# A two-layer graph attention kernel: streamed weights, block loads and weight negations moved in the queues of its first superblock

## The chip, the cores and the metric

The kernel runs on one core of one Trainium2 chip. The metric is the device time of one execution in microseconds; a comparison takes the median of several. In the profile, PE is TensorE (PEld its weight loads), DVE is VectorE, ACT is ScalarE, POOL is GpSimd and SP is SyncE, whose queue (SPq) issues nearly all DMAs. "L530" is line 530 of the kernel before.

## The reference

`x` is 128 graphs of 64 nodes with 768 features, in float32; `adj` is 128 symmetric 64x64 masks with ones on the diagonal. Cut to what matters:

```python
h = relu(layernorm(x))
for l in range(2):
    m_left, m_right = h @ W_left[l].T, h @ W_right[l].T
    u_left  = einsum('bih,bjh->bij', h, m_left) / sqrt(768)
    u_right = einsum('bih,bjh->bij', h, m_right) / sqrt(768)
    u = u_left * triu(adj) + u_right * triu(adj, 1).T
    e = exp(u) * adj
    attention = e / (sum(e, axis=2) + 1e-10)
    ctx = attention @ (h @ W_lin[l].T + b_lin[l])
    h = relu(layer_norm(ctx, ln_a[l], ln_b[l]))
out = x + h
```

## The kernel before

**Tiling.** The 8192 tokens are cut into 16 blocks of 512 (four pairs of graphs on each half), two blocks form a superblock, so there are 8 superblocks. For each layer two passes run. Pass one computes the projections with W_left and W_right and, from them, the scores and the softmax, which it stores in DRAM as the transposed attention. Pass two computes the projection with W_lin, then the context, its norm and either the next layer's rows (layer 1, stored in DRAM) or the output (layer 2).

**The products.** Both passes multiply by a scheme of fast matrix multiplication (blocks of 256 by 256): pass one has 29 products for a superblock (`PRODUCTS`, index i from 0 to 28) instead of 36. Each product takes a sum of weight blocks, made by `W_OPS`, and a sum of token blocks, made by `X_OPS` on GpSimd (token index 12 and up). Each product has two runs of eight matmuls, k = 0 for the left weights and k = 1 for the right ones. A run takes about 1.73 us. Results are accumulated in PSUM banks X, Y, Z for k = 0 and V, right0, right1 for k = 1, and read into the tile `m` (`read`, L293): the first time an output block appears ScalarE copies it (L303), later VectorE adds (L221). A bank may not be written again until its reads have run.

**The weights.** In superblock 0 of layer 1 the weight sums are made while the products run: those of the left on VectorE, most of those of the right on GpSimd (`weight_op`, L180 to L186). `W_OPS` has two negations for each side, weights 16 and 27, used by products 7 and 20. The sums lie in tiles that are free at the time, handed out by `Singles`: a list of groups, each with a limit; a tile of a group takes only weights whose last use is at or before the group's limit. After product i its two weights are kept in DRAM (`keep_weight`, L194). From superblock 1 on the weights are streamed (L197) from there into a ring of 8 tiles of 512 KB, each an l and r pair. The first five streamed tiles go into ring tiles that superblock 0 uses for single weights, so they can't start before these are dead (L698 to L700). Later streams are sent by `streamed` (L554), and around the scores they are held back (`HELD`, and a small copy on ScalarE at L558 that the next stream waits for), so that the DMA queue is quiet while the scores run.

**The rows.** Layer 1's blocks 0 and 1 come in by TensorE transposes. For blocks 2 and up `load_rows` (L360) loads rows of `x`; `transpose_rows` (L384) then queues four statistics on VectorE (L338, L339), the scale (ScalarE L407, VectorE L408 and L409), four normalisations with Relu on ScalarE (L412) and four 32x32 transposes on VectorE (L397), then the store to DRAM (L394). `load_h` (L371) brings the block back with features on the partitions. Block 3 is written out by hand (L731 to L740), since the first half of its rows has a tile of its own.

**The order.** It is written out by hand. A superblock of pass one has 116 slots: four for each product (after the first four matmuls and at the end of the two runs: slots 4i, 4i+1, 4i+2, 4i+3). `put(slot, f)` plans f for a slot, `put_all` a list of them with a step, and `run(slot)` issues what is planned; a slot with nothing planned takes the next of the `idle` list. Within an engine instructions run in the order of issue. SyncE issues DMAs in program order too, and as it runs nothing else it is often ahead of TensorE. `starts` (L751 to L755) gives the slots at which the two next blocks begin.

**The scores.** `scores` (L460, L472) multiplies the tokens of a block by `m`: 192 short matmuls of 32 columns of weights into the bank `both`. In superblock 1 those of block 0 come after product 0, those of block 1 after product 2. The chain of a block's softmax (`chain`, L476 to L512) is cut into steps by `yield`: mask products on VectorE (L488), their sum (L492), Exp on ScalarE (L494), the row sums and the division (L496 to L502), a transpose (L506) and eight small stores. At the end of pass one the last block's chain is planned into the first slots of pass two (L793), beside the first products of `linear` (L1049, L1063).

**Layer 2.** Its pass one takes the right banks from the memory that pass two of layer 1 used for its context, so product 0's second run waits for the last norm of that pass (L1032, L1034).

## Time and profile before

| | us |
|---|---|
| median of 3 runs | 2712.75 |
| lowest, highest | 2711.25, 2714.27 |
| the profiled execution | 2710.28 |
| its span | 2708.5 |

The stretches of the span, with the busy time of each engine in it:

| stretch, us | what runs | PE | DVE | ACT | POOL | DMA share |
|---|---|---|---|---|---|---|
| 0 to 10 | load, first transposes | 7.12 | 5.50 | 5.04 | 1.05 | 0.84 |
| 10 to 60 | layer 1, superblock 0 | 47.96 | 38.77 | 27.80 | 31.64 | 0.87 |
| 60 to 130 | the same, and the start of superblock 1 | 64.32 | 49.39 | 4.08 | 47.47 | 0.78 |
| 130 to 240 | superblock 1 | 107.91 | 69.83 | 25.62 | 37.41 | 0.87 |
| 240 to 780 | superblocks 2 to 6 | 539.10 | 320.77 | 134.52 | 204.15 | 0.72 |
| 880 to 910 | end of pass one, start of pass two | 27.72 | 18.94 | 6.36 | 25.12 | 0.13 |
| 910 to 1330 | layer 1, pass two | 420.00 | 153.52 | 200.10 | 258.54 | 0.56 |
| 1330 to 1380 | its end, start of layer 2 | 48.11 | 13.58 | 26.67 | 18.28 | 0.73 |
| 1380 to 2200 | layer 2, pass one | 819.87 | 429.64 | 171.72 | 309.87 | 0.72 |
| 2650 to 2709 | the end | 47.40 | 42.80 | 18.39 | 35.98 | 0.55 |

PE's busy time is read against the length of the stretch: where the two agree, nothing but the matmuls sets the pace. The granted clock of TensorE is 0.999. A line of the timeline gives the start in us, the duration in us, the engine, the line, the operation, what it writes and reads, how many are merged, and in brackets the idle time of the engine just before and what ended it. Tiles bear the names of the memory they lie in: a weight sum in superblock 0 can be `wp` (a ring tile), `ht`, `room`, `bias` or `ts`.

### The profile page before, as it was taken

How to read it: one execution, taken by the hardware profiler on the slowest of the kernel's cores; microseconds unless marked ns; L12 is line 12 of the kernel's file. 1: busy time of each engine (PE TensorE's matmuls, PEld its weight loads, DVE VectorE, ACT ScalarE, POOL GpSimd, SP SyncE). 2: the span in 40 equal slices, each digit the busy share in tenths (PEclk: the TensorE clock that was granted, in tenths of full speed). 3: DMA queues.
4: the chain of work that ended last, by engine and by line, in shares of the span. 5: the costliest groups of instructions: out<-in, count | busy, mean ns of one | idle time of the engine just before them, and what ended most of it. 6: DMA issues, size and time to landing. Idle time of an engine off the chain costs nothing.

```text
span 2708.5 us, 47300 instructions
## 1 busy us (share of the span) xinstructions
PE 2677.3 (99%) x18514; PEld 2304.5 (85%) x18514; DVE 1502.9 (55%) x2458; ACT 829.2 (31%) x1615; POOL 1380.6 (51%) x1071
## 2 busy tenths in 40 slices
PE   9899999999999999999999999999999999999998
PEld 7788888888888888888788888888888888888886
DVE  7665655756647433334343645546446475666667
ACT  4032131321310254454631221221212304445443
POOL 5633244333336776566433325334244286887886
PEclk9999999999999999999999999999999999999999
DMA  8886966858765345558585956958759524655655
GB/s 268 273 304 208 286 204 205 280 203 263 243 209 179 98 144 180 169 168 259 180 279 176 308 190 220 283 185 287 227 194 302 211 79 133 185 157 159 185 156 148
DMA packets 310223, 567.81 MB, mean 210 GB/s; under 512 B 62833, under 2 KB 190065, under 8 KB 301809
## 3 DMA queue, kind: packets, MB, share of 16 engines
q1 hardware_dynamic: 309840, 564.39, 65.1%
q8 instruction: 148, 2.42, 0.4%
q14 instruction: 75, 0.61, 0.1%
q10 hardware_dynamic: 160, 0.39, 0.0%
HBM read 429.40 MB, written 135.27 MB: 208 GB/s over the span
## 4 chain that ended last, share of the span: by engine, by line
PE 94%; DVE 2%; DMA 1%; SPq 1%; issue 0%; ACT 0%; DVEq 0%
PE right L530 17%; PE X L1063 12%; PE X L530 11%; PE V L530 10%; PE Z L530 9%; PE Y L530 9%; PE V L1063 8%; PE Y L1063 6%; PE both L472 5%; PE Z L1063 4%; PE aux L871 2%; PE aux L894 1%; PE Y L894 0%; DMA wp<-ws 0%; PE Z L472 0%
## 5 line engine op out<-in xcount | busy, mean ns | idle before, releaser
L221 POOL TENSOR_TENSOR ts<-ht 128x512 f32<-128x512 f32 x352 | 479.7, 1369 | 160.7 <-PE X L1063 65.9
L221 POOL TENSOR_TENSOR ts<-ht,ts 128x512 f32<-128x512 f32 x192 | 253.0, 1325 | 348.5 <-PE V L530 208.2
L530 PE MATMUL right<-ts,wp 128*128 128x252 f32 (+1 forms) x1632 | 381.1, 377 | 1.5 <-DVE wp L221 1.5
L530 PEld LDWEIGHTS right<-ts,wp 128*128 128x128 f32 x1632 | 310.5, 190 | 40.0 <-DVE wp L221 1.9
L481 POOL TENSOR_TENSOR wm<-adj,tri 128x256 f32<-128x256 f32 x60 | 42.2, 726 | 493.9 <-DMA wp<-ws 220.7
L221 DVE TENSOR_TENSOR m<-m,X 128x512 f32<-128x512 f32 x160 | 105.6, 685 | 259.6 <-ACT m L303 181.3
L221 DVE TENSOR_TENSOR m<-m,right 128x504 f32<-128x504 f32 (+1 forms) x304 | 199.5, 673 | 87.5 <-PE right L530 73.5
L1063 PE MATMUL X<-room,ts 128*128 128x256 f32 x1024 | 244.1, 380 | 0.2
L221 POOL TENSOR_TENSOR ts<-ht,ht 128x512 f32<-128x512 f32 x128 | 163.5, 1288 | 140.0 <-PE right L530 93.7
L530 PE MATMUL Z<-ts,wp 128*128 128x256 f32 x992 | 234.5, 380 | 0.1
L1063 PEld LDWEIGHTS X<-room,ts 128*128 128x128 f32 x1024 | 192.0, 190 | 31.3 <-issue 1.8
L530 PEld LDWEIGHTS Z<-ts,wp 128*128 128x128 f32 x992 | 188.8, 190 | 24.8 <-issue 0.4
L530 PE MATMUL X<-ts,wp 128*128 128x256 f32 x872 | 207.5, 381 | 0.0
L530 PE MATMUL V<-ts,wp 128*128 128x252 f32 (+1 forms) x864 | 201.7, 377 | 0.0
L303 ACT ACTIVATE m<-right 128x504 f32<-128x504 f32 (+1 forms) x64 | 36.1, 590 | 510.2 <-PE both L472 490.3
L380 ACT ACTIVATE ht<-ht,b_col,a_col 128x512 f32<-128x512 f32 x192 | 140.8, 803 | 144.0 <-DMA ht<-h 144.0
L530 PEld LDWEIGHTS X<-ts,wp 128*128 128x128 f32 x872 | 164.9, 190 | 22.8
L1063 PE MATMUL Y<-room,ts 128*128 128x256 f32 x768 | 182.6, 380 | 0.0
L530 PEld LDWEIGHTS V<-ts,wp 128*128 128x128 f32 x864 | 164.4, 190 | 20.2
L1063 PEld LDWEIGHTS Y<-room,ts 128*128 128x128 f32 x768 | 146.1, 190 | 20.1 <-issue 0.6
L221 DVE TENSOR_TENSOR m<-m,Y 128x512 f32<-128x512 f32 x144 | 95.8, 683 | 115.1 <-PE Y L530 104.6
L1029 POOL TENSOR_TENSOR z<-z,b 128x768 f32<-128x768 f32 x62 | 112.6, 1830 | 89.8 <-DVE z L1026 89.8
(225 smaller groups left out, 4845.0 us busy)
## 6 DMA issues: line engine op xcount, KB each, us to landing
wp<-ws SPq DMA_DIRECT2D x435, 512.0 KB, 6.4
ht<-h SPq DMA_DIRECT2D x62, 1536.0 KB, 8.7
h<-room SPq DMA_DIRECT2D x112, 384.0 KB, 6.9
z<-z SPq DMA_DIRECT2D x128, 192.0 KB, 3.1
ws<-wp SPq DMA_DIRECT2D x93, 256.0 KB, 4.4
xr<-in_x_dram SPq DMA_DIRECT2D x120, 192.0 KB, 3.6
out_dram<-xr SPq DMA_DIRECT2D x120, 192.0 KB, 2.6
room<-z SPq DMA_DIRECT2D x112, 192.0 KB, 5.2
```

The lines of the kernel that those rows point to most:

```text
L221: (eng.tensor_add if sign == "+" else eng.tensor_sub)(o, a, b)
L303: nc.scalar.activation(to(o), p, AF.Copy, scale=1.0 if sign == "+" else -1.0)
L380: nc.scalar.activation(ht, ht, AF.Relu, bias=cols[1][:, c:c + 1], scale=cols[0][:, c:c + 1])
L472: nc.tensor.matmul(p[h * S + e:h * S + e + 32, q, e:e + 95], ht[:, c, b * S + e:b * S + e + 32], mb[:, e:e + 95], start=(c == 0), stop=(c ...
L481: nc.gpsimd.tensor_tensor(wm[:, :, k], adj[:, :, 1 - k], tri[:, k].unsqueeze(1).to_broadcast([P, Q, S]), op=ALU.mult)
L530: nc.tensor.matmul(p[:, g], wk[:, c, g * P:(g + 1) * P], tk[:, c, :].rearrange("p (b s) -> p b s", s=S)[:, :, :ns], start=(new and g == c ...
L871: nc.tensor.matmul(cx[k][i, m, :HH], at[j, q, :], hl[j, q, m * HH:(m + 1) * HH], start=True, stop=True)
L894: nc.tensor.matmul(parts[r, k][n][i], at[j, q, :], hl[j, q, cut], start=True, stop=True)
L1029: nc.gpsimd.tensor_add(zs[k], zs[k], rows["b"])
L1063: nc.tensor.matmul(p[:, n], b[t][:, c, r * P:(r + 1) * P], w[s][:, c, :], start=(i in FIRST and i not in PRELOAD and n == c == 0), stop=(c ...
```

## The change

Seven edits, all in the order of work or in the engine that does it; what is computed stays.

1. A negation planned for VectorE goes to ScalarE. The two of the right weights stay on GpSimd.
2. Block 2's four transposes on VectorE stand two slots apart instead of one. Its store and the second half of block 3's rows, planned behind them, so move from slots 51 and 52 to 55 and 56.
3. Streamed tiles 0 and 1 of superblock 1 are issued after product 23 instead of 25. For that the four half tiles they go to move into the group with limit 23, and some weights get other tiles: stream 0's tile now holds weight 19 (product 23) in place of weight 3 (product 22).
4. The loads of blocks 2 and 3 are planned at slots 85 and 98 instead of 92 and 101.
5. The rows of block 4 move from slot 112 of superblock 0 to slot 12 of superblock 1. There blocks 4 and 5 start at slots 18 and 60 instead of 8 and 52, and the stores of blocks 0 and 1 for pass two move from slots 20 and 26 to 26 and 34.
6. In superblock 0 of layer 2 the order of the first runs is product 0 left, product 1 left, product 0 right, product 1 right.
7. The last block's softmax steps in pass two stand at slots 6 and 9 (sum, Exp) and 12 to 22, instead of 3 to 15.

```diff
         t = ss.take((kind, o), LAST_W[o])
         if sign != "neg":
             added(eng, t, sign, ss[kind, a], ss[kind, b])
+        elif eng is nc.vector:
+            nc.scalar.mul(t, ss[kind, a], -1.0)
         else:
             eng.tensor_scalar_mul(t, ss[kind, a], -1.0)
...
         for f in moved:
             todo.append(f)
-            todo.extend(none * (l or u >= 4))
+            todo.extend(none)
...
-                for i, (w, t, at, new, what) in enumerate(PRODUCTS):
-                    for k in range(2):
+                steps = [(i, k) for i in range(NP) for k in range(2)]
+                if l and not U:
+                    steps[1], steps[2] = steps[2], steps[1]
+                for n, (i, k) in enumerate(steps):
+                    w, t, at, new, what = PRODUCTS[i]
...
-                ss = Singles(((20, chunks(2)), (23, chunks(3)), (25, early),
+                ss = Singles(((20, chunks(2)), (23, chunks(3) + early[:4]), (25, early[4:]),
...
-                    if i == 25:
-                        for n in range(5):
-                            stream(0, NP + n)
+                    for n in {23: (0, 1), 25: (2, 3, 4)}.get(i, ()):
+                        stream(0, NP + n)
...
                 if l == 0 and U == 1:
+                    put(12, lambda: load_rows(l, 4))
                     for n in range(2):
-                        put(20 + 6 * n, lambda n=n: nc.sync.dma_start(KEPT[0][n], HT[1, 0, n]))
+                        put(26 + 8 * n, lambda n=n: nc.sync.dma_start(KEPT[0][n], HT[1, 0, n]))
...
                             put(87, store)
-                            put(SLOTS - 4, lambda: load_rows(l, 4))
-                            put(101, lambda: load_h(1, l, u))
+                            put(98, lambda: load_h(1, l, u))
...
-                        slot = max(slot + 15, 92) if U == 0 and l == 0 else slot + 15
+                        slot = max(slot + 15, 85) if U == 0 and l == 0 else slot + 15
...
-                        starts = (8, 52) if U else (26, 56)
+                        starts = ((26, 56), (18, 60))[U] if U < 2 else (8, 52)
...
-            put_all(3, two[2:])
+            put_all(put_all(6, two[2:4], 3), two[4:])
```

In `project` the loop over i and k becomes one over the list of steps; slots are counted by the place n of a step in it, and a product's tiles are freed, and `done(i)` is called, after its right run.

More of the change, by code (lines that the diff above doesn't have):

```diff
@@ L519, in project @@
                 bank, seen, late = {}, (set(), set()), []
-                for i, (w, t, at, new, what) in enumerate(PRODUCTS):
-                    for k in range(2):
-                        ns = S - 1 if k and U < NU - 1 else S
-                        if new:
-                            bank[k, at] = (right[at - 1] if k and at else
-                                           ps_st.tile([P, 2 * TH], F32, name="V" if k else "XYZ"[at]))
-                        p = bank[k, at][:, :NBB * ns].rearrange("p (g b s) -> p g b s", g=2, s=ns)
-                        wk, tk = weights(i, k), tokens(l, U, t)
-                        for g in range(2):
-                            for c in range(K2):
-                                nc.tensor.matmul(p[:, g], wk[:, c, g * P:(g + 1) * P],
-                                                 tk[:, c, :].rearrange("p (b s) -> p b s", s=S)[:, :, :ns],
-                                                 start=(new and g == c == 0), stop=(c == K2 - 1),
-                                                 skip_group_check=True)
-                            if g == 0:
-                                run(4 * i + 2 * k)
-                        late.append((k, p, ns, what))
-                        if k and i in TURNS:
-                            if U:
-                                scores(2 * U - 2 + TURNS[i], both[TURNS[i]])
-                            M[2 * U + TURNS[i]] = sp.tile([P, C, NBB, 2, S], F32, name="m", bufs=2)
-                        now, late = late[::-1], []
-                        for kk, pp, n, todo in now:
-                            if any(2 * U + int(o, 16) % 4 // 2 not in M for o in todo[1::2]):
-                                late.append((kk, pp, n, todo))
-                                continue
-                            read(pp, lambda o: M[2 * U + o % 4 // 2][:, o // 4 * K2:(o // 4 + 1) * K2,
-                                                                     o % 2 * 4:o % 2 * 4 + 4, kk, :n], todo, seen[kk])
-                        run(4 * i + 2 * k + 1)
-                    for n, last in LAST_X.items():
-                        if last == i and n >= 12:
-                            free((l, U, n))
@@ new lines, in project @@
+                steps = [(i, k) for i in range(NP) for k in range(2)]
[3 more added lines that the diff above has]
+                    w, t, at, new, what = PRODUCTS[i]
+                    ns = S - 1 if k and U < NU - 1 else S
+                    if new:
+                        bank[k, at] = (right[at - 1] if k and at else
+                                       ps_st.tile([P, 2 * TH], F32, name="V" if k else "XYZ"[at]))
+                    p = bank[k, at][:, :NBB * ns].rearrange("p (g b s) -> p g b s", g=2, s=ns)
+                    wk, tk = weights(i, k), tokens(l, U, t)
+                    for g in range(2):
+                        for c in range(K2):
+                            nc.tensor.matmul(p[:, g], wk[:, c, g * P:(g + 1) * P],
+                                             tk[:, c, :].rearrange("p (b s) -> p b s", s=S)[:, :, :ns],
+                                             start=(new and g == c == 0), stop=(c == K2 - 1),
+                                             skip_group_check=True)
+                        if g == 0:
+                            run(2 * n)
+                    late.append((k, p, ns, what))
+                    if k and i in TURNS:
+                        if U:
+                            scores(2 * U - 2 + TURNS[i], both[TURNS[i]])
+                        M[2 * U + TURNS[i]] = sp.tile([P, C, NBB, 2, S], F32, name="m", bufs=2)
+                    now, late = late[::-1], []
+                    for kk, pp, size, todo in now:
+                        if any(2 * U + int(o, 16) % 4 // 2 not in M for o in todo[1::2]):
+                            late.append((kk, pp, size, todo))
+                            continue
+                        read(pp, lambda o: M[2 * U + o % 4 // 2][:, o // 4 * K2:(o // 4 + 1) * K2,
+                                                                 o % 2 * 4:o % 2 * 4 + 4, kk, :size], todo, seen[kk])
+                    run(2 * n + 1)
+                    if not k:
+                        continue
+                    for o, last in LAST_X.items():
+                        if last == i and o >= 12:
+                            free((l, U, o))
```

## The prediction

> **What bounds the kernel now.** I read the page first, then the waits of TensorE by stretches, then the timelines of TensorE, VectorE and SyncE around each wait, then the DMA issues in narrow windows.

> The page, engine totals:

> ```profile
> PE 2677.3 (99%) x18514; PEld 2304.5 (85%) x18514; DVE 1502.9 (55%) x2458; ACT 829.2 (31%) x1615; POOL 1380.6 (51%) x1071
> ```

> TensorE is the bound: only 2708.5 - 2677.3 = 31.2 us of the span are not matmul time, some 11.6 of them in the tail that the change doesn't touch. The matmuls are the same before and after, so the gain must come from the idle gaps. The timeline of TensorE shows the five that the change aims at and one that it may touch (start, duration, in brackets the idle time before it and its releaser):

> ```profile
> 60.55 1.97 PE L530 MATMUL right<-ts,wp 128*128 128x252 f32 x8 [1.46 <-DVE wp L221]
> 88.64 1.97 PE L530 MATMUL Y<-ts,ht 128*128 128x256 f32 x8 [1.82 <-DVE ht L186]
> 122.30 1.97 PE L530 MATMUL Y<-ht,wp 128*128 128x256 f32 x8 [2.58 <-DMA wp<-ws]
> 132.09 1.02 PE L472 MATMUL both<-m,ht 128*32 128x95 f32 x38 [2.75 <-issue]
> 901.73 1.97 PE L1063 MATMUL X<-room,ht 128*128 128x256 f32 x8 [1.39 <-ACT hl L303]
> 1363.12 1.94 PE L530 MATMUL right<-ht,wp 128*128 128x252 f32 x8 [1.34 <-DVE z L1032]
> 2235.92 1.97 PE L1063 MATMUL X<-room,ht 128*128 128x256 f32 x8 [0.67 <-ACT hl L303]
> ```

> The rest is VectorE's order in the first superblock. Its timeline:

> ```profile
> 59.84 0.65 DVE L221 TENSOR_TENSOR wp<-wp,wp 128x512 f32<-128x512 f32 x1
> 60.41 0.97 DVE L397 STREAM_TRANSPOSE room<-room 128x768 f32<-128x768 f32 x1
> ...
> 77.15 1.00 DVE L338 BATCH_NORM_STATS2 st<-room 128x6 f32<-128x384 f32 x2
> ...
> 81.77 1.18 DVE L221 TENSOR_TENSOR wp<-ht 128x512 f32<-128x512 f32 x1
> ...
> 87.19 1.30 DVE L186 TENSOR_SCALAR ht<-wp 128x512 f32<-128x512 f32 x1
> ```

> and SyncE's:

> ```profile
> 104.56 0.47 SPq L373 DMA_DIRECT2D ht<-h  x1
> 105.08 2.29 SPq L194 DMA_DIRECT2D ws<-wp  x4
> 107.41 0.50 SPq L373 DMA_DIRECT2D ht<-h  x1
> 108.00 0.93 SPq L194 DMA_DIRECT2D ws<-wp  x2
> 112.93 8.73 SPq L197 DMA_DIRECT2D wp<-ws  x5
> ```

> SyncE's DMAs name eight completion semaphores in turn, and each waits until the one eight places earlier has landed. So the first streamed tile (112.93, landing 122.16) waits for a 1.5 MB block load issued at 104.56 (landing 112.87).

> [...] a weight sum takes 0.65 us at 59.84, before GpSimd starts at 60.63, and 1.15 and 1.76 us at 61.30 and 62.37 beside it. [...] the 128x512 copies at L303 took 0.59. [...] such a block came at 129.61, inside the 2.75 us gap, while the DMA engines were full.

> **The change, part by part.** A product is two 1.73 us runs.

> *Negations.* The first (36.47, 0.72 us on VectorE) frees nothing: two operations later VectorE reads bank Z, which TensorE fills until 37.62, and before it was there at 37.70. The second is priced below, in its chain.

> *Transposes two slots apart.* VectorE ran sum (54.84), transpose, sum, transpose, bank read, sum, transpose, sum (59.84), transpose. Now the third transpose falls behind the last sum of these four: it ends at 60.49 - 0.89 = 59.6, and TensorE's 1.46 shrinks by 0.9. The next two sums find GpSimd half a turn off, so product 14 starts about 1.0 earlier (65.1 for 66.10). The 0.67 us at 57.13 stays.

> The price: the fourth transpose ends later, about 62.8 for 61.38 (bounds 61.9 and 64.1 by how the sums alternate with GpSimd). On SyncE the store of block 2 waits for it, and the half of block 3's rows stands behind: before, four stores from 61.45, two kept weights, rows issued by 71.78 and landed at 76.92. The slots of store and rows move by four, so the kept weights of product 12 go ahead and those of 13 take their place; the rows land at 76.92 + 1.45 = 78.4. VectorE reaches their statistics (77.15 before) at 76.15, and its queue is in order: it stands for 2.3 us. Behind it are four bank reads, the other statistics and the sum that ended at 82.95, now 84.25. Product 19 needs it (83.23 before), so starts at 84.35. Then the reads, the scale and the last sum end at 88.35 (87.09 before); the negation takes 0.6 to 0.75 on ScalarE in place of 1.30 on VectorE; product 20 starts at 89.1 for 88.64. Net: 0.5 later. Bounds: 1.8 earlier if the rows land in time, 1.5 later at the other end. ScalarE's four normalisations wait behind the negation, but VectorE reaches their transposes no sooner.

> *Streams and block loads.* Behind product 20 TensorE ran 31.08 us without a gap to 119.72; now to 120.2. Block 2 is loaded at slot 85, behind product 20's kept weights (91.3), while SyncE waits for block 3's transposes anyway (store at 95.0, as before). Stream 0's tile now held the weights of product 23, so it waits for their landing, near 109.4 (the kept weights of 22 landed at 107.90, each 0.8 after the last); it lands near 113 to 115, and block 3's load, behind it, near 119 to 120, needed only by product 1 at 127.7. The 2.58 goes: the second superblock starts at 120.2 for 122.30, **2.1 us gained** (bounds -1 and 4). What is late next is nothing up to the scores.

> *Rows of the fifth block.* They leave the DMA queue ahead of the scores (124.20 to 132.13) and come behind the four held tiles (146.57 to 147.94). The second superblock keeps the DMA engines at 99% or more from 150 on, so their 1.5 MB push what follows by 4 to 5 us; the streams have 6.7 to 20 us in hand. But the statistics stand at slot 18 in VectorE's queue: the first half lands at about 157.9 by the pace of the tiles (1.35 us per 512 KB) and rows (0.7 per 192 KB), and behind them are product 4's reads, which product 7 needs at 159.83. They end at 160.3: **0.6 us lost** (0 to 2.5). Blocks 4 and 5 ten and eight slots later, and the masks behind their adjacency loads on GpSimd (2.7 late where 7.7 are in hand), cost nothing.

> *The gap in the scores (2.75).* With two streams, three products' kept weights and one more tile behind them, some 3 MB, the engines are still full near 124.3, when I expect that block to be wanted. I take 0; bounds: 2.75 gained, 1 lost.

> *Order of the first steps of layer 2.* Product 1's first run is put into the 1.34 us wait, and its bank and tile are free. Product 1 ends at 1366.65 for 1368.33 on that count: **1.65 us gained** (0 if its bank were also held).

> *Last block's softmax.* The Exp stood ahead of the bank copy that product X waits for. Moved to slot 9, that copy can run at 898.65, and X starts at 900.18 for 901.73: 1.55; in layer 2, 2235.09 for 2235.92: 0.83. The eleven later steps lie beside 20 us of matmuls with VectorE 40 to 60% busy. **2.4 us gained** (2.0 to 2.4).

> **Sum:** 2.1 - 0.6 + 0 + 1.65 + 2.4 = 5.55. Against the profiled execution: 2710.28 (span 2708.5 and 1.8 around it) - 5.55 = 2704.7. That execution lies 2.5 below the median shown, so I put the forecast at 2712.75 - 5.55 = 2707.2.

> **Rivals.**
> - *The score gap goes too.* For: the rows are out of the queue, and it drains near 130 rather than 140. Against: it is still full at the start of the scores. Then 2707.2 - 2.75 = 2704.5.
> - *The first superblock gives nothing.* Block 3's rows or the kept weights of product 23 use up the 2.1. For: stream 0 stands behind a landing that it did not wait for before. Then 2709.3.
> - *Slower: block 3's rows hold VectorE.* Place: the statistics at 77.15; each microsecond after 78.4 reaches product 19 one for one, and the whole is a loss from a landing at about 84. For: the store ahead of them took 10.3 us (61.45 to 71.73) for 1.5 MB; if it took twice that, they land at 88.7 and the time is 2707.2 + 10.3 = 2717.5. Against: the engines were idle before it in both orders.

> **How the numbers follow.** Forecast 0.52, score gap gone 0.20, nothing in the first superblock 0.17, slower 0.11. The likeliest one's own range is 2705 to 2709.7 (its bounds on the first superblock and the rows). I widen to 2702.5 and 2711.5 for the second and third cases and the 3 us between runs. 0.2% is 5.4 us, about what a measurement of this kernel can tell from no change, and the forecast lies on that line: half of the first case, nearly all of the second and a little of the third make 0.51 faster; slower 0.11 is the last; the rest, 0.38, within.

> **What would show it.** Right: no wait for wp<-ws ahead of the second superblock, none for hl in either second pass, none for z at layer 2's start; VectorE idle some 2 us for rows before the statistics near 77; product 20 near 89; a wait of product 7 in the second superblock of 0 to 2.5 us. Wrong: statistics without a wait (then 2 us better), a wait for wp<-ws at 120, the score gap below 1 us, or new waits of TensorE after 165 in the second superblock.

## The result, and the profile after

The changed kernel takes 2728.11 us, median of 6 runs (2727.37 to 2733.51), against 2712.0 (2710.04 to 2714.27) for the kernel before on the same chip: a ratio of 1.0062, 95% interval 1.0049 to 1.0075. It is slower by about 16 us, where 5.5 us of gain were forecast. Its profiled execution has a span of 2726.0 us, 17.5 more than the 2708.5 of before.

The engine totals of the page after:

```profile
PE 2684.6 (98%) x18514; PEld 2305.4 (85%) x18514; DVE 1495.5 (55%) x2456; ACT 830.9 (30%) x1617; POOL 1380.5 (51%) x1071
```

The same 18514 matmuls are busy for 7.3 us longer than before, which no wait can do: part of the loss is matmuls that themselves run slower, so the forecast's premise that the matmuls are the same before and after, and only idle gaps count, did not hold. The rest is idle time. To place it, the start of each run of matmuls was set against the start of the same run before. "Offset" is after minus before, "step" what the offset changed by since the row above:

| place in the kernel | before | after | offset | step |
|---|---|---|---|---|
| superblock 1 starts | 122.30 | 120.97 | -1.33 | -1.3, first superblock |
| product 3 | 144.29 | 144.27 | 0.0 | +1.3, in the first scores |
| product 9 | 164.96 | 175.75 | +10.8 | +10.8, ahead of and in products 7 and 8 |
| product 18 | 195.80 | 213.52 | +17.7 | +6.9, ahead of and in product 17 |
| superblock 2, after its first scores | 241.47 | 261.88 | +20.4 | +2.7, in those scores |
| product X of pass two's start, layer 1 | 901.73 | 920.90 | +19.2 | -1.2: 1.55 gained by the softmax, 0.3 lost ahead of it |
| layer 2, product 2's left run | 1368.33 | 1385.85 | +17.5 | -1.65: 1.6 gained by the order of steps |
| product X, layer 2 | 2235.92 | 2253.36 | +17.4 | -0.1: 0.84 gained by the softmax, 0.76 lost ahead of it |

(The small losses ahead of the softmax lie in short gaps of the scores in between.) So the late parts of the change do what was forecast, the first superblock gives its gain away in the scores that follow, and nearly all of the loss, 17.7 us, lies in two stretches of the second superblock of layer 1. The timeline of TensorE after, around both and at the gap in the third superblock's scores (start, duration, in brackets the idle time before and its releaser):

```profile
158.08 1.89 PE L535 MATMUL X<-ts,wp 128*128 128x256 f32 x8
162.44 1.97 PE L535 MATMUL V<-ts,wp 128*128 128x252 f32 x8 [2.46 <-DVE m L223]
169.42 3.78 PE L535 MATMUL X<-ht,wp 128*128 128x256 f32 x8 [5.02 <-ACT m L305]
173.00 2.91 PE L535 MATMUL V<-ht,wp 128*128 128x252 f32 x8
...
207.42 3.78 PE L535 MATMUL Y<-ht,wp 128*128 128x256 f32 x8 [4.10 <-DVE m L223]
211.00 2.69 PE L535 MATMUL right<-ht,wp 128*128 128x252 f32 x8
...
261.58 0.36 PE L474 MATMUL both<-m,ht 128*32 128x95 f32 x5 [2.74 <-issue]
```

The reader is to see two things. Product 7's right run waits 2.46 us for a bank read of VectorE, product 8 waits 5.02 for a copy of ScalarE, product 17 waits 4.10 for VectorE. And behind the two long waits the same eight matmuls take 3.78 us where they took 1.89 (161.53 before, same form). What VectorE did there:

```profile
151.34 1.29 DVE L223 TENSOR_TENSOR m<-m,X 128x512 f32<-128x512 f32 x2 [28.90 <-ACT m L305]
159.98 1.02 DVE L340 BATCH_NORM_STATS2 st<-room 128x6 f32<-128x384 f32 x2 [7.36 <-DMA room<-in_x_dram]
...
166.78 0.21 DVE L341 BATCH_NORM_AGGREGATE mv<-st 128x2 f32<-128x12 f32 x1
...
193.08 0.68 DVE L223 TENSOR_TENSOR m<-m,right 128x504 f32<-128x504 f32 x1 [1.01 <-PE right L535]
205.55 1.02 DVE L340 BATCH_NORM_STATS2 st<-room 128x6 f32<-128x384 f32 x2 [11.79 <-DMA room<-in_x_dram]
```

It stands at the first statistics of block 4 for 7.36 us and at those of block 5 for 11.79 us, each time for the rows, with finished banks behind it in its queue. ScalarE:

```profile
151.43 1.56 ACT L305 ACTIVATE m<-V 128x504 f32<-128x504 f32 x3
167.03 0.30 ACT L409 ACTIVATE sd<-mv,eps_in 128x4 f32<-128x4 f32 x1 [14.04 <-DVE mv L341]
...
168.80 0.58 ACT L305 ACTIVATE m<-X 128x512 f32<-128x512 f32 x1
```

The square root of the deviations (167.03) needs the fourth aggregate (166.78). It stands in ScalarE's queue ahead of the copy of product 7's bank X (168.80, at 160.03 before), for which product 8 waits. So the late rows hold two engines, one after the other. SyncE:

```profile
148.36 8.55 SPq L370 DMA_DIRECT2D room<-in_x_dram  x8
...
188.43 0.57 SPq L514 DMA_DIRECT2D att<-wm  x1
...
191.89 4.58 SPq L396 DMA_DIRECT2D h<-room  x4
...
198.51 4.67 SPq L370 DMA_DIRECT2D room<-in_x_dram  x8
```

Block 4's rows are issued from 148.36; their first half landed at 159.90. Block 5's are issued from 198.51 (173.56 before), behind the first attention store, for which SyncE had stood since 179.73, and behind block 4's store. And the first scores of the second superblock after:

```profile
124.48 3.37 PE L474 MATMUL both<-m,ht 128*32 128x95 f32 x153
130.32 1.47 PE L474 MATMUL both<-m,ht 128*32 128x95 f32 x39 [2.46 <-issue]
131.72 3.18 PE L535 MATMUL Z<-ht,wp 128*128 128x256 f32 x8
```

The gap behind the 153rd matmul is 2.46 us for 2.75, but this time the run behind it takes 3.18 us for 2.00: the 1.3 us gained ahead of it are gone.

### The profile page after: what moved, and what is told of

It is laid out like the page before. It is cut to its first block, busy times and chain, and to the rows that moved or that the text cites. A ratio compares the mean times of both kernels' runs of the same rounds, so it can differ in the third digit from the quotient of the medians.

```text
span 2726.0 us, 47301 instructions
## 1 busy us (share of the span) xinstructions
PE 2684.6 (98%) x18514; PEld 2305.4 (85%) x18514; DVE 1495.5 (55%) x2456; ACT 830.9 (30%) x1617; POOL 1380.5 (51%) x1071
## 3 DMA queue, kind: packets, MB, share of 16 engines
q8 instruction: 148, 2.42, 0.4%
## 4 chain that ended last, share of the span: by engine, by line
PE 94%; DVE 2%; SPq 1%; DMA 1%; issue 0%; ACT 0%; DVEq 0%; ACTq 0%
PE right L535 17%; PE X L1069 12%; PE X L535 11%; PE V L535 10%; PE Z L535 9%; PE Y L535 9%; PE V L1069 8%; PE Y L1069 6%; PE both L474 5%; PE Z L1069 4%; PE aux L877 2%; PE aux L900 1%; DMA room<-in_x_dram 1%; PE Y L900 0%; DVE m L223 0%
## 5 line engine op out<-in xcount | busy, mean ns | idle before, releaser
L1069 PEld LDWEIGHTS Y<-room,ts 128*128 128x128 f32 x768 | 145.8, 190 | 20.4 <-issue 0.6
L223 DVE TENSOR_TENSOR hl<-hl,V 128x512 f32<-128x512 f32 (+1 forms) x136 | 89.1, 655 | 128.9 <-PE V L1069 118.7
```

What stands on the lines that cost most here:

```text
L223: (eng.tensor_add if sign == "+" else eng.tensor_sub)(o, a, b)
L1069: nc.tensor.matmul(p[:, n], b[t][:, c, r * P:(r + 1) * P], w[s][:, c, :], start=(i in FIRST and i not in PRELOAD and n == c == 0), stop=(c ...
```

## The experiments

Twelve kernels were run. All times are medians, and each ratio, with its 95% interval, is to runs of the kernel before that stand beside that kernel's on the same chip; the medians of before lay between 2712.14 and 2714.30.

### Which part loses: the rows put back, and the rows alone

The changed kernel without the move of the rows:

```diff
-                    put(12, lambda: load_rows(l, 4))
-                        put(26 + 8 * n, lambda n=n: nc.sync.dma_start(KEPT[0][n], HT[1, 0, n]))
+                        put(20 + 6 * n, lambda n=n: nc.sync.dma_start(KEPT[0][n], HT[1, 0, n]))
...
                             put(87, store)
+                            put(SLOTS - 4, lambda: load_rows(l, 4))
...
-                        starts = ((26, 56), (18, 60))[U] if U < 2 else (8, 52)
+                        starts = (8, 52) if U else (26, 56)
```

> The changed kernel with the rows of the fifth block, the starts of blocks 4 and 5 and the two stores of kept blocks put back where they were. Theory (VectorE and ScalarE stand in order at the statistics of blocks 4 and 5, and TensorE behind them): the 10.8 and 6.9 us lost at products 8 and 17 of the second superblock go, and nothing else of the change was harmful, so 2706 to 2711 us, with no TensorE gap over 1 us between 140 and 235 us; the new 2.7 us gap in the scores near 260 goes too, because the DMA queue is back in its old order there. Rival (the first superblock's edits harm what follows, or the half-speed clock is a state of the chip and not a follower of the gaps): 2720 or more.

Measured: 2708.46 us (15 runs), ratio 0.9983 (0.9976 to 0.9991), as the theory had it. TensorE has no wait from 140 to 235 us, and none in the third superblock's first scores.

The kernel before with the move alone:

> The kernel before with nothing changed but the rows of the fifth block behind the held tiles, the starts (18, 60) and the two stores. Theory: it loses the same two stretches, 15 to 21 us, so 2727 to 2733 us, with gaps of 4 to 6 us ahead of product 8 and product 17 of the second superblock and half-speed runs behind them. Rival (it takes the earlier streams too, so that the queue is in another order): less than 8 us lost, under 2720.

Measured: 2731.09 us (5 runs), ratio 1.0064 (1.0050 to 1.0078). Its waits of TensorE from 140 to 240 us:

```profile
PE X L530 <- ACT m L303: 5.4, 1, 5.4
PE Y L530 <- DVE m L221: 3.7, 1, 3.7
PE V L530 <- DVE m L221: 1.9, 1, 1.9
```

(Us in total, times, longest.) They are the three of the changed kernel, followed by the same 3.78 us runs. The move of the rows, with the slots moved along with it, carries the whole loss and makes it without the other edits: the first superblock isn't its cause.

### The place in the DMA queue, or the place of the statistics

The changed kernel with the rows left behind the held tiles, and the statistics later, six slots for block 4 and two for block 5:

```diff
-                        starts = ((26, 56), (18, 60))[U] if U < 2 else (8, 52)
+                        starts = ((26, 56), (24, 62))[U] if U < 2 else (8, 52)
```

> The changed kernel with the rows where the change put them, but block 4 starting at slot 24 instead of 18 and block 5 at 62 instead of 60. Theory (the place of the statistics in the queues decides, not the place of the rows in the DMA queue): the gap ahead of product 8 goes (0 to 1 us left of 10.8), block 5 still stands and costs 0 to 7: 2709 to 2718 us. Rival (1.5 MB of rows in the full stretch of the DMA queue are what costs, through the streams behind them): 2724 or more, with TensorE waiting for streamed tiles.

Measured: 2721.63 us (6 runs), ratio 1.0030 (1.0019 to 1.0042). The total is 3.6 above the expected band, since block 5 cost more than I allowed; the question is answered by block 4. VectorE, ScalarE and TensorE there:

```profile
160.56 1.02 DVE L340 BATCH_NORM_STATS2 st<-room 128x6 f32<-128x384 f32 x2 [3.60 <-DMA room<-in_x_dram]
```

```profile
161.44 0.60 ACT L305 ACTIVATE m<-X 128x512 f32<-128x512 f32 x1 [7.02 <-PE X L535]
...
166.68 0.30 ACT L409 ACTIVATE sd<-mv,eps_in 128x4 f32<-128x4 f32 x1 [2.94 <-DVE mv L341]
```

```profile
161.24 1.86 PE L535 MATMUL V<-ts,wp 128*128 128x252 f32 x8
162.94 1.89 PE L535 MATMUL X<-ht,wp 128*128 128x256 f32 x8
```

The rows land as late as in the changed kernel, and VectorE still stands 3.60 us for them. But the reads of products 4 and 5 now come before the statistics in its queue, and the copy of product 7's bank comes before the square root in ScalarE's. Products 7 and 8 (161.24, 162.94) start without a wait: all 10.8 us of the first stretch are gone. What costs there is what stands behind the waiting instruction. TensorE waited for no streamed tile. At block 5 it waited 7.70 us in one piece, with a half-speed run behind it.

### Block 5: slots, or SyncE's queue

The changed kernel with the rows of block 4 put back ahead of the scores, but the later starts and stores kept:

```diff
-                    put(12, lambda: load_rows(l, 4))
...
                             put(87, store)
+                            put(SLOTS - 4, lambda: load_rows(l, 4))
```

> The changed kernel with the rows of the fifth block back ahead of the scores, but the later starts (18, 60) and the later stores kept. Theory: nothing at block 4 (its rows are there 20 us early), and at block 5 a stand of VectorE of 2 to 6 us, of which TensorE sees 0 to 3: 2708 to 2714 us. Rival (the ten and eight slots themselves cost, by the queue of SyncE, in which block 5's rows are moved behind the attention stores): the whole 6.9 us of the second stretch stay, 2714 to 2719.

Measured: 2717.71 us (20 runs), ratio 1.0020 (1.0013 to 1.0026), which is the rival's band. Nothing is lost at block 4, and the second stretch is whole:

```profile
198.68 3.78 PE L535 MATMUL Y<-ht,wp 128*128 128x256 f32 x8 [3.92 <-DVE m L223]
```

Now with one more edit, the rows of block 5 six slots sooner:

```diff
-                            put(slot + 7, lambda: load_rows(l, u + 1, halves=(1,) if (l, u) == (0, 2) else (0, 1)))
+                            put(slot + (1 if (l, u) == (0, 4) else 7), lambda: load_rows(l, u + 1, halves=(1,) if (l, u) == (0, 2) else (0, 1)))
```

> The run with the later starts alone, but the rows of block 5 issued at slot 45, ahead of the attention stores and of block 4's store on SyncE's queue, in place of slot 51 behind them. Theory (the second stretch is lost because the move put these rows behind the attention stores, which wait for the softmax): they are issued near 175 to 180 for 189.9, land before 190, and VectorE does not stand or stands under 2 us: no gap over 1 us ahead of product 17, 2709 to 2712 us for 2717.7. Rival (the slots themselves, VectorE's own backlog): 2715 or more.

Measured: 2713.18 us (12 runs), ratio 0.9998 (0.9990 to 1.0007). SyncE with the later starts alone, and then with the rows ahead:

```profile
179.87 0.57 SPq L514 DMA_DIRECT2D att<-wm  x1
...
189.93 4.67 SPq L370 DMA_DIRECT2D room<-in_x_dram  x8
```

```profile
175.35 5.87 SPq L370 DMA_DIRECT2D room<-in_x_dram  x8
181.71 0.57 SPq L514 DMA_DIRECT2D att<-wm  x1
```

And VectorE, in the same order:

```profile
196.80 1.02 DVE L340 BATCH_NORM_STATS2 st<-room 128x6 f32<-128x384 f32 x2 [11.61 <-DMA room<-in_x_dram]
```

```profile
186.36 0.68 DVE L223 TENSOR_TENSOR m<-m,right 128x504 f32<-128x504 f32 x1 [1.01 <-PE right L535]
186.96 1.01 DVE L340 BATCH_NORM_STATS2 st<-room 128x6 f32<-128x384 f32 x2
```

With the same slots for the statistics the stand of 11.61 us is gone, and TensorE has no gap near product 17. So the second stretch comes from SyncE's order: ten slots later, block 5's rows fall behind the attention stores, the first of which waits for the end of a softmax, and so behind block 4's store. The total is 1.2 above the band; this run's gap in the first scores is 4.54 us, of which the next part tells.

### The gap in the scores

The rows at slot 4 of the second superblock, with the old starts and stores:

```diff
-                    put(12, lambda: load_rows(l, 4))
+                    put(4, lambda: load_rows(l, 4))
```

> The changed kernel with the rows of the fifth block at slot 4 of the second superblock (ahead of the held tiles, into the stretch from 136 to 146 us in which the DMA engines stood idle in the changed kernel), and the old starts (8, 52) and stores. Theory: the rows land by 141, the statistics stand in VectorE's queue while nothing is behind them, no gap over 1 us from 140 to 235; the gap in the scores ends near 130.3 as in the changed kernel and not at 132.2 as with the rows put back, so 1.5 to 2.5 us under that run: 2706 to 2707 us. Rival (any place behind the scores costs, since the held tiles then come later): 2710 or more, with TensorE waiting for streamed tiles near 144 to 160.

Measured: 2709.3 us (21 runs), ratio 0.9983 (0.9977 to 0.9990): the same ratio as with the rows put back, so the 1.5 to 2.5 us that the theory promised over that run did not come. There is no gap from 140 to 235 us, but the first scores have one of 4.26 us, not 2.46. A slot sets an order and no time: SyncE issued these rows from 132.49, right behind the last weights, with the gap still running to 135.10.

The same, and two early tiles moved from the first superblock's end to slot 1:

```diff
-                    for n in {23: (0, 1), 25: (2, 3, 4)}.get(i, ()):
+                    for n in {23: (0, 1), 25: (2,)}.get(i, ()):
...
+                    put(1, lambda: stream(0, NP + 3), lambda: stream(0, NP + 4))
                     put(4, lambda: load_rows(l, 4))
```

> The same, and the fourth and fifth early streamed tiles (1 MB) taken out of the queue ahead of the scores and issued at slot 1 of the second superblock. Theory (the gap in the scores is a block of instructions that comes late because the DMA queues are full; its end, not its length, is fixed by the queue): the gap ends 1 us or more earlier, so it shrinks from about 2.5 to under 1.5 us and the half-speed run behind it goes: 2703 to 2705.5 us. Rival (the gap has another cause, or the queue is as full without the two tiles): gap 2 us or more, same time as the run with slot 4, within 1 us.

Measured: 2707.13 us (11 runs), ratio 0.9974 (0.9966 to 0.9983). The time lies between the two bands, and the theory's sign for it failed: the gap is 3.15 us, though no half-speed run follows it. SyncE had again run ahead, and issued the tiles from 124.57 and the rows from 127.03, so the queue was as full as before (a DMA share of 1.07 and 1.05 from 126 to 130 and from 130 to 134 us, for 0.90 and 1.05 in the changed kernel).

So the next two runs tie the issue to the scores. ScalarE writes one column of the fourth tile behind its first bank copy after the first scores, and SyncE's load of that tile has to wait for it (with the two tiles out of the first superblock, as above):

```diff
+                    def behind_scores():
+                        nc.scalar.copy(RING[(NP + 3) % RINGS][:, 0, 0, :1], eps_in)
+                        for n in (3, 4):
+                            stream(0, NP + n)
+
+                    put(3, behind_scores)
```

In the first, `put(5, lambda: load_rows(l, 4))` follows, with the old starts. In the second, the rows stay behind the held tiles, with the starts (24, 62) and block 5's rows ahead of the attention stores.

> The run with the two tiles taken out, but now they, the sixth tile and the rows wait on SyncE for a one-column copy that ScalarE makes behind its first copy of a bank after the first scores (near 133 us); in the runs before, SyncE had run ahead and issued them into the scores. Old starts (8, 52). Theory (the gap in the scores is an instruction block queued behind full DMA queues): the first scores run with a gap under 1 us for 2.5 to 4.5, and without the half-speed run behind; the 3 MB now fill 130 to 142 us, so a gap of 1 to 3 us may come in the second scores (137 to 142) in its place: 2703 to 2707 us. Rival (the gap comes with the scores themselves, whatever is in the queue): gap of 2 us or more in the first scores, 2706 to 2710.

> The changed kernel with the fourth to sixth tile behind the first scores as in the run beside it, the rows of the fifth block left behind the held tiles, block 4 starting at slot 24, block 5 at 62, and block 5's rows issued ahead of the attention stores. Theory: no gap over 1 us in either scores, no gap over 2 us at products 8 and 15 to 17; with the gains of the later parts 2703 to 2706.5 us, so 0.2 to 0.35% under the kernel before. Rival (rows behind the held tiles cost in any place): 2710 or more.

Measured: 2712.38 us (13 runs), ratio 0.9990 (0.9982 to 0.9999), a miss, above both bands; and 2707.28 us (10 runs), ratio 0.9976 (0.9967 to 0.9986), 0.8 above its band. TensorE in the first, both scores:

```profile
126.14 3.37 PE L474 MATMUL both<-m,ht 128*32 128x95 f32 x153
131.66 1.02 PE L474 MATMUL both<-m,ht 128*32 128x95 f32 x39 [2.14 <-issue]
...
148.28 0.44 PE L474 MATMUL both<-m,ht 128*32 128x95 f32 x8 [4.65 <-issue]
148.65 3.56 PE L535 MATMUL X<-ts,wp 128*128 128x256 f32 x8
```

and in the second:

```profile
128.83 1.02 PE L474 MATMUL both<-m,ht 128*32 128x95 f32 x39 [1.13 <-issue]
...
136.83 4.34 PE L474 MATMUL both<-m,ht 128*32 128x95 f32 x192
```

The DMA share of the stretches 126 to 130, 138 to 142 and 142 to 146 us (last columns: granted clock, DMA share, GB/s), first run and then second:

```profile
126.00:130.00 4.00, 3.52 (x155) 3.24 (x154) 0.00 (x0) 0.00 (x0) 3.92 (x4) 1.00 0.91 344
...
138.00:142.00 4.00, 4.00 (x125) 3.54 (x127) 0.00 (x0) 1.19 (x2) 1.33 (x2) 1.00 1.04 303
142.00:146.00 4.00, 1.62 (x80) 1.41 (x72) 1.80 (x5) 0.00 (x0) 0.00 (x0) 1.00 1.01 218
```

```profile
126.00:130.00 4.00, 2.87 (x122) 2.59 (x114) 0.00 (x0) 0.09 (x1) 3.92 (x4) 1.00 0.17 64
...
138.00:142.00 4.00, 3.99 (x151) 3.56 (x141) 0.00 (x0) 0.76 (x2) 0.00 (x0) 1.00 0.01 4
```

The second scores are the clean comparison. With the engines full there (1.04 and 1.01) the first kernel waits 4.65 us; with them empty (0.01) the second has no gap at the same place. The first scores say less. The two programs are still the same there; the second's trace reaches them 1.8 us sooner, so that the stretch from 126 to 130 us lies later in them, and its last transfer queued ahead of them lands 4.06 us after their start (128.38) where the first's lands 4.98 after (131.12). Its gap is 1.13 us for 2.14.

The DMA records show what moves in the gap: a 16 KB block of instructions (the kernel before has 148 of them, 2.42 MB in all; the one that the forecast names, at 129.61, is among them), which lands shortly before TensorE goes on. It landed at 130.39 and 146.95 for 131.66 and 148.28, at 127.47 for 128.83, and in the kernel before and the changed one at 130.53 and 128.84 for 132.09 and 130.32; in the first scores of all fourteen kernels it is 1.2 to 1.6 us. So the gap is most likely a block of instructions that queues with the data: the wait was 4.65 us with the engines at 1.04 and 1.01 and none at 0.01. A finer order is not shown, since 1.07 and 1.05 went with 3.15. No run moved the block's border by itself. I expected the gap to move to the second scores, but sized it at 1 to 3 us where it was 4.65, with a half-speed run behind it.

What the runs do not show is the theory's other half, that the queue fixes the end of the gap. The kernel before and the one with the later parts alone (below) are the same program up to 880 us, and their last rows land at 137.80 and 137.77. Yet the first starts its scores at 125.89 and goes on at 132.09, the second at 127.33 and 134.45: a later start, and a later end. The length of this gap also differs from one execution to the next where the program up to it is the same: 2.75 and 3.66 us in these two, 2.46 and 3.58 in the changed kernel and the one with late statistics, 3.24, 3.79 and 4.54 with the later starts alone, the rows put back and the rows of block 5 ahead. One trace beside another can't place a microsecond here.

### The remaining parts alone

The two last edits on the kernel before:

> The kernel before with the last two edits alone: the order of layer 2's first steps and the last block's softmax. Theory: the traces of the change show 1.65, 1.24 and 0.61 us gained there, 3.5 in sum, and nothing before 880 us moves: 2708 to 2709.2 us (about 2712.1 less 3.5). Rival (the gains are taken back downstream or depend on the delayed queue): 2710.5 or more.

Measured: 2710.11 us (19 runs), ratio 0.9986 (0.9979 to 0.9993). The medians differ by 3.4 (2713.52 for before on that chip), for 3.5 expected. (That took 1.24 and 0.61 us for the softmax, which have the small losses ahead of it in them; by its own steps it is 1.55 and 0.84, and 4.0 with the order.) The absolute band, worked out from another chip's 2712.1, is missed by 0.9.

The run with the rows put back, less the transposes and negations:

```diff
-        elif eng is nc.vector:
-            nc.scalar.mul(t, ss[kind, a], -1.0)
...
-            todo.extend(none)
+            todo.extend(none * (l or u >= 4))
```

> The run with the rows put back, and the transposes and negations of the first superblock put back too: of the first superblock's edits only the earlier tiles and block loads stay. Theory (the forecast's own steps: the 2.58 us wait goes by the loads alone, the transposes give 0.9 at product 12 and lose it by product 20): the second superblock starts 2.0 to 3.0 us sooner than before where the start of the trace is taken off, the 1.46 us wait ahead of product 12 and the 1.82 ahead of product 20 are back; the scores still end where the queue lets them, so 2707 to 2710 us. Rival (the transposes were what made the second superblock early): a start within 1 us of before.

Measured: 2707.31 us (10 runs), ratio 0.9975 (0.9966 to 0.9984). Its scores:

```profile
120.28 1.89 PE L533 MATMUL Y<-ht,wp 128*128 128x256 f32 x8
...
131.45 1.80 PE L472 MATMUL both<-m,ht 128*32 128x95 f32 x38 [4.20 <-issue]
```

It starts the superblock 2.0 us sooner than the kernel before (122.30) and 1.2 sooner than the run with all of the first superblock's edits (121.52); the waits of 1.46 and 1.82 us ahead of products 12 and 20 are back. So the loads make the gain, and the transposes and negations cost 1.2 of it. Beside the traces of before and of all the edits the gain seems lost again, since the scores go on at 131.45 for 132.09 and 132.20. But beside the run of the later parts, which has the first superblock of before and was timed on the same chip, the superblock starts 1.8 us sooner (122.08), the scores go on 3.0 sooner (134.45), and the median is 2.8 lower (2710.11). The two ratios' intervals overlap, so it is open how much of the gain stays.

The last run is the one with the tiles behind the first scores and the rows behind the held tiles, less the same two edits:

> The run with the tiles behind the first scores, the rows behind the held tiles and the statistics late enough, less the transposes and negations of the first superblock (which the two runs with and without them put at 1.2 to 1.3 us of its start). Theory: the second superblock starts another 0.5 to 1.3 us sooner, the first scores keep their gap of about 1 us and the third ones their 2.3, so 2705.5 to 2707 us. Rival (the score gap ends where the queue lets it, so that an earlier start only lengthens it): no gain, 2707 to 2708.5.

Measured: 2707.38 us (12 runs), ratio 0.9980 (0.9971 to 0.9988). Its second superblock starts at 119.71, 1.1 sooner than with the edits, and none of it is seen in the time, as the rival had it, though 1.1 us is less than the intervals can tell. Its third superblock's first scores have a gap of 2.49 us and a half-speed run behind. Three other runs, the two tiles at slot 1, the paced tiles with held rows, and the loads alone, have ratios of 0.9974 to 0.9976: all four beat both kernels, and their intervals don't tell them apart.

## Why the prediction was wrong

The forecast was 2707.2 (2702.5 to 2711.5), the time is 2728.11. By the terms of its sum, in the profiled executions (a minus is a gain):

| term | forecast | measured |
|---|---|---|
| first superblock, streams and block loads | -2.1 | -1.3 |
| gap in the scores, and the run behind it | 0 | +1.3 |
| rows of the fifth block | +0.6 | +10.8 |
| blocks 4 and 5 ten and eight slots later | 0 | +6.9 |
| third superblock's scores | not named | +2.7 |
| order of the first steps of layer 2 | -1.65 | -1.6 |
| last block's softmax | -2.4 | -2.4 |
| short gaps in other scores | not named | +1.0 |

**The step that failed is the rows of the fifth block.** It had the mechanism for its first half: the statistics stand at slot 18 in VectorE's queue, and product 4's reads behind them are needed by product 7. The first half landed at 159.90 for 157.9. I had priced the rows at 0.7 us per 192 KB behind tiles that land when they did before; in the trace the fourth held tile lands at 156.58 for 154.72, since it shares the engines with the rows (99% busy from 148.3 to 157 us), and the rows come 0.9 us apart. That alone makes the wait of product 7 2.46 us, within the bound of 2.5 that I gave.

What I left out is what follows. I stopped at the first reader. The fourth aggregate runs at 166.78, ScalarE's square root waits for it, and the copy of bank X stands behind the square root: 5.02 us more, on another engine than the one I was watching. The run with the statistics six slots later shows it, with rows as late and no loss. And I priced a wait at its length. TensorE's matmuls behind it ran at half speed, which made 2.9 of the 10.8 us and 2.7 of the 6.9. My own sign of being wrong came true here: new waits of TensorE after 165, at 169.42 and 207.42.

**The second failed step is the sentence that blocks 4 and 5, ten and eight slots later, cost nothing.** I looked at the slots' distance to the loads and the masks, and not at the queue that the rows of block 5 are moved past: in the kernel before they are issued at 173.56, ahead of the attention stores; ten slots later they are behind them, and a softmax's end on VectorE sets when they start. The run with these rows at slot 45 shows it by taking the whole stretch away.

**The rival on the other side** had this mechanism, VectorE standing at statistics for rows, but at block 3 in the first superblock, where the rows landed at 79.49 (forecast 78.4) and VectorE stood 2.41 us (2.3). At block 4 the rows had all landed by 137.80 before, 13 us ahead of the next bank read (151.36); that margin was spent by the move, and I had priced only an excess of 0.6.

**The first superblock** went much as worked out: product 12 waits 0.59 (0.56 forecast), product 19 starts at 85.08 (84.35), product 20 at 90.05 (89.1), for ScalarE and no longer for VectorE, the first streamed tile lands at 113.78 (113 to 115), block 3's load at 120.95 (119 to 120), the superblock starts at 120.97 (120.2). Of the 0.8 missing, 0.44 is at the trace's start, where product 0 starts later. One reading failed: the 0.67 us at 57.13, said to stay, became 1.38 at 58.07, so that product 12 starts at 60.63 for 60.55: 0.4 sooner with the later start of the trace taken off, and not 0.9. That the next sums would meet GpSimd at another time was my estimate from the three sums that the forecast names: product 14 starts at 65.92 for 65.1 (66.10 before), and beside GpSimd the sums at 61.99 and 64.25 take 0.87 and 1.52 us. The second negation takes 0.63 us on ScalarE (estimated 0.6 to 0.75). The 1.3 us lost in the scores are not the gap, which is 0.3 shorter, but the half-speed run behind it, and that is chance: it hangs on where the gap falls, as the last section shows, and the traced execution of before happens to have none. The rival in which the gap goes was right in its reason, the full DMA engines, and didn't happen: they were still full at 126 to 130 us (0.90), as I had judged.

**The later parts** were right. Layer 2's order gave 1.6 us for 1.65, and the softmax 1.55 and 0.84 for 1.55 and 0.83; on the kernel before alone they gave 3.4 by the medians.

**The third superblock's gap** of 2.7 us was not foreseen. It is there in all seven kernels in which block 5 starts at slot 60 or 62 and in none of the seven in which it starts at 52 is there one over 0.45 us. A block of instructions lands there too, 1.5 us before TensorE goes on (260.11 for 261.58). Which of the delayed transfers holds it up was not tried.

## What to carry to other kernels

Before a load is moved later, follow every instruction that waits for it to the end of its chain, and for each engine of the chain write down what stands behind the waiting instruction: the loss begins there, and moving the waiting instruction behind those reads can be the whole cure (here of 10.8 us). A slot in an issue order is no time: SyncE's queue ran ahead of the compute here (rows at slot 4 issued at 127.03, into the first scores) or stood behind a store that waited (from 179.73 to 188.43), so look at what the moved issue passes on its own queue, and tie it to an event if it must not come sooner. A trace is one execution: before a microsecond is explained, look for two executions of the same program at that place, and see how far they differ.

## What the runs showed of the hardware

```profile
127.32:130.73 3.41, 0.95 (x46) 0.81 (x41) 0.00 (x0) 0.00 (x0) 3.33 (x4) 1.00 0.93 310
130.73:134.15 3.42, 3.42 (x36) 2.70 (x26) 0.00 (x0) 1.08 (x2) 3.34 (x4) 0.50 1.05 409
```

```profile
127.24:130.65 3.41, 2.10 (x99) 1.89 (x91) 0.00 (x0) 0.00 (x0) 3.33 (x4) 1.00 1.05 399
130.65:134.06 3.41, 1.97 (x43) 1.72 (x43) 0.00 (x0) 0.90 (x2) 3.25 (x4) 1.00 1.06 247
```

The gap of 2.46 us lies in one piece of the grid, and the next piece runs at half the clock. The longer gap of 2.75 us straddles a border, 1.31 and 1.44 us, and nothing follows. In the changed kernel the pieces with 3.41, 2.50 and 2.46 us of idle time have half the clock behind them; in the kernel before the most is 1.88, and none has. The fourteen traces, from 15 us to the tail, have 10970 such pieces at full clock. The next one was at half after all 21 in which TensorE idled 2.05 us or more, and after none of the 10949 in which it idled 1.90 us or less. At half clock, 1.14 us of idle time or more kept the next piece at half too (seven cases), and 0.46 or less ended it (21 cases). So each of the six gaps of 3.68 to 7.70 us ahead of a product brought two pieces at half clock, in which matmuls of 128x256 started 0.42 to 0.43 us apart in place of 0.212 to 0.216, and it cost 1.9 to 2.9 us more than its length. Gaps of 2.1 to 3.2 us had it or not: 3.15 us in one run had nothing behind it, 2.08 us in two others did. Ahead of the tail the changed kernel has 17.1 us at half clock, the traced execution of before none, and that of the later parts, the same program up to 880 us, 6.8. I had not put any of this into a price.

The fetch of instructions can be seen in the time. TensorE stood 2.14 us where a 16 KB block came through DMA engines with a share of 0.91, and 4.65 us where it was 1.04 and 1.01, in scores whose small matmuls pass 153 of their number in 3.4 us, and not at all at the same place in the second scores when the engines were empty (0.01).
